# A gated graph network and an attention layer on one core: a split by a scaled rounding copy, tanh gates, a three-pass projection, and right-hand scores by way of DRAM

## The chip, the core and the metric

The kernel runs on one core of a Trainium2 chip. The metric is the device time of one execution in microseconds (us), the median of a few runs. TensorE (PE) does the matrix products, VectorE (DVE) and ScalarE (ACT) the elementwise work, GpSimd (POOL) little, and SyncE (SP) issues nearly all DMAs. Each engine works through its own queue in order.

## The reference, cut to what matters

There are 64 graphs of 256 nodes with 256 features. The first layer is a gated network of three rounds, the second an attention layer; both work on a normalised input and add to it.

```python
h = jnp.maximum(_layernorm(x, axis=-1), 0.0)
for i in range(3):                                   # gated network
    m = jnp.einsum('bnd,de->bne', h, weight[i])
    aggr = jnp.einsum('bst,bsd->btd', A, m)          # A = (adj != 0)
    gi = aggr @ w_ih.T + b_ih;  gh = h @ w_hh.T + b_hh
    r = sigmoid(i_r + h_r);  z = sigmoid(i_z + h_z)
    n = tanh(i_n + r * h_n)
    h = (1.0 - z) * n + z * h
x = x + h
h = jnp.maximum(_layernorm(x, axis=-1), 0.0)
hW = jnp.einsum('bnd,od->bno', h, W)                 # attention
e = (hW @ a_left)[:, :, None] + (hW @ a_right)[:, None, :]
e = where(adj == 0, -1e9, leaky(e))
x = x + softmax(e) @ hW
```

## The kernel before

**Pairs.** Two graphs make a pair, so that the free size of a tile is 512 columns (two graphs of 256 nodes) on 128 partitions; 32 pairs follow each other. In the gated network the features are on partitions (`hT`, two blocks `db`), in the attention layer the nodes are.

**Set-up.** `setup` (L325) transposes the weights, multiplies `weight[i]` into `w_ih`, and splits each gate matrix into three factors `fac` (`factors`, L372): a top part cut to few mantissa bits, the remainder scaled by 4096, and a correction. `wT` is W transposed, in plain float32. `va` holds W^T times the two halves of `a`, so that the attention scores are dot products with `h` itself.

**A round.** `split` (L445) takes a value apart in the same way: a cut by a bit mask on DVE (`cut`, L322), a rounding copy of the cut value on ACT (L449), the remainder on DVE (L450) and a combination of both on DVE (L451). The three parts are float32r tiles ("round" buffers). Propagation (`prop`, L584) multiplies two-part features with A into a PSUM bank; ACT copies the bank to SBUF (L588) and `split` works on the copy. `gate` (L455) then makes each gate's bank in two steps: "top" matmuls with the first two parts (L464), a scaling of the bank by 1 + 1/4096 on ACT (L478), and "rest" matmuls with the third part (L469). ACT applies the sigmoid for r (L599) and z (L610) and the tanh for n (L607); DVE multiplies r into the bank (`u`, L603), adds (L606), and mixes old and new h (L615 to L617). A DMA transpose (`dma_turn`, L489, with gathers at L494, and a joining copy on ACT at L502) brings h back to nodes on partitions for the next propagation, where `hi` (L641) and `lo` (L642) split it in two.

**The attention layer.** DVE makes the score dot products (L656) into columns of a small tile. The right-hand scores, one per node and so one per partition, are needed along the free axis on every partition: PE transposes each column, broadcast to 128 columns, into a bank `pR` (`right`, L667). ACT adds the left-hand score and applies the leaky slope (L671), DVE masks (L674) and takes the row maximum (L676). One planned operation `exps` (L679) makes the exponentials of both graphs (L683), with the sums. The result is transposed by DMA (on PE in the last pair), PE multiplies h by it (`mix`, L714, plain float32), ACT copies the bank (L718), PE multiplies by `wT` (`project`, L723, plain float32), DVE scales by the softmax sum and adds the residual (L728), and SP stores.

**The order.** A planner (`Plan`) gets every operation with its engine, an estimated occupation and latency, and the buffers that it reads and writes. It simulates the engines and emits one order for each engine's queue by least start time, then by due time, which the dictionary `LEAD` shifts by name. Buffers come from classes: "full" (28 float32 tiles), "round" (32), and "bank" (8 PSUM banks) among them. A window of four pairs may be in work at once.

Of the kernel before, what the change touches and what calls it, by code (L numbers as in the profile page):

```python
# [27 lines left out]
    "w load": 28000, "w copy": -12000, "w cut": -5000, "w 1": -17000, "w copies": -7000, "G": -9000, "G copy": -5400,  # L28
    "va copy": 4000, "in 0 stats": 5000, "in 1 relu": 10000, "turn copy 0": -11800, "h0 0": 17000, "h0 d": 13000,
    "h1 0": 36000, "prop 0": 11200, "g0 cut": 3000, "g1 cut": 13000, "g1 0": -28000, "r 0 topT": 51000,  # L30
    "r 0 rest": -4300, "r 0": 29000, "ni 0 rest": 46000, "z 0 topF": -48000, "z 0": 11000, "d mul 0": -19000,
    "r 1 topT": -34000, "r 1 rest": -1000, "nh 1 topF": -42000, "nh 1 scale": -38000, "nh 1 rest": 3000,
    "ni 1 topF": -24000, "tanh 1": 10000, "z 1 topF": -61000, "z 1 scale": -112000, "z 1": 6000, "back 0": -36000,
    "hi 0": 28000, "back copy 1": -67000, "hi 1": 52000, "mid 0 stats": -14000, "right 0": -8000,
    "mid 1 eps": -23000, "mid 1 relu": 9000, "dot 1": -31000, "mix 0": -28000, "p copy 1": 40000,
    "project 1": -6000, "turn 1 gather": 2000,
# [16 lines left out]
class Plan:  # L53
# [6 lines left out]
    def __init__(self, window, lead):  # L60
        self.ops, self.slots, self.window, self.pair = [], {}, window, -1
        self.writer, self.readers = {}, {}
        self.due = None
        self.stage = None
        self.lead = lead
        self.keep = {"full": 0, "round": 0}
# [4 lines left out]
    def op(self, name, eng, occ, lat, fn, r=(), w=(), ahead=0, port=False):  # L71
# [3 lines left out]
        o.stage, o.name, o.lead = self.stage, name, self.lead.get(name, 0)  # L75
# [125 lines left out]
def tile_gated_gnn_then_gat(  # L201
# [34 lines left out]

    nc = tc.nc
# [16 lines left out]
    plan.slot_class("full", [const.tile([P, GN], F32, name=f"full{i}") for i in range(28)])  # L254
# [4 lines left out]
    plan.slot_class("bank", [psum.tile([P, GN], F32, name=f"bank{i}") for i in range(8)])  # L259

# [28 lines left out]
    A512, V512, S512, VP256, C512 = 475, 605, 660, 392, 522  # L289
    CUT = -4096  # L290
    SPLIT = 4096.0
    C = 1.0 / SPLIT

# [4 lines left out]
    b_rz = const.tile([P, EB], F32, name="b_rz")  # L298
    b_i = vec[:, 2 * DB : 2 * DB + EB]
# [3 lines left out]
    wT = const.tile([P, DB, D], F32, name="wT")  # L303
# [21 lines left out]
    def setup():  # L325
# [16 lines left out]
        dve("b_rz", 70, lambda: nc.vector.tensor_add(b_rz, b_i, b_h), r=[("vec", ONE)], w=[("b_rz", ONE)])  # L342

# [10 lines left out]
        def transposed(dst, region, blocks):  # L354

            def go_for(c):
                pt = Buf("bank")

                def go():
                    for r, (b, k) in enumerate(blocks):  # L360
                        nc.tensor.transpose(pt.t[:, ts(r, P)], parts(b)[:, k, ts(c, P)], ident)

                n = len(blocks)
                pe("w turn", TR * n, go, r=[(b, ONE) for b, _ in blocks] + [("ident", ONE)], w=[(pt, ONE)])
                act("w copy", 140 + n * 110, lambda: nc.scalar.copy(dst(c), pt.t[:, : n * P]), r=[(pt, ONE)], w=[region(c)])

            for c in range(DB):
                go_for(c)

        H = E3 // 2  # L370

        def factors(m, T):  # L372

            def one(kb, half):
                f = lambda j: fac[m][:, j, kb, ts(half, H)]
                b, t = T[kb][half], Buf("full")
                src, top = lambda: b.t[:, :H], lambda: t.t[:, :H]
                key = (f"fac{m}", ((kb, half),))
                cut("w cut", top, src, H, [(b, ONE)], [(t, ONE)])
                dve2("w 1", 460, lambda: nc.vector.tensor_sub(src(), src(), top()), r=[(t, ONE)], w=[(b, ONE)])  # L380

                def copies():
                    nc.scalar.copy(f(0), top())
                    nc.scalar.activation(f(1), src(), AF.Copy, scale=SPLIT)

                act("w copies", 800, copies, r=[(b, ONE), (t, ONE)], w=[(f"fac{m}", ((kb, half, 0),))])
                dve2("w d", 510, lambda: nc.vector.scalar_tensor_tensor(f(2), top(), -C, src(), op0=ALU.mult, op1=ALU.add),
                    r=[(b, ONE), (t, ONE)], w=[(f"fac{m}", ((kb, half, 1),))])

            for half in range(2):  # L390
                for kb in range(DB):
                    one(kb, half)
# [4 lines left out]
        def whole(T, blocks):  # L397
            for half in range(2):
                transposed(lambda c, half=half: T[c][half].t[:, :H], lambda c, half=half: (T[c][half], ONE),
                           blocks[3 * half : 3 * half + 3])  # L400
# [4 lines left out]
        whole(whhT, whh_n)  # L405
# [24 lines left out]
        transposed(lambda c: wT[:, c, :], lambda c: ("wT", (c,)), W_n)  # L430
# [12 lines left out]
    WT = [("wT", (0, 1))]  # L443

    def split(name, v):  # L445

        t, v0, v1, vd = Buf("full"), Buf("round"), Buf("round"), Buf("round")
        cut(name + " cut", lambda: t.t, lambda: v.t, GN, [(v, ALL)], [(t, ONE)])
        act(name + " 0", C512, lambda: nc.scalar.copy(v0.t, t.t), r=[(t, ONE)], w=[(v0, ONE)])  # L449
        dve2(name + " 1", V512, lambda: nc.vector.tensor_sub(v1.t, v.t, t.t), r=[(v, ALL), (t, ONE)], w=[(v1, ONE)])  # L450
        dve2(name + " d", V512, lambda: nc.vector.scalar_tensor_tensor(vd.t, v1.t.bitcast(F32), -SPLIT, t.t, op0=ALU.mult, op1=ALU.add),  # L451
            r=[(v1, ONE), (t, ONE)], w=[(vd, ONE)])
        return v0, v1, vd

    def gate(name, e, terms, tops, apart=False, bias=0.0):  # L455
# [22 lines left out]
        act(name + " scale", 575 if "nh" in name else A512, lambda: nc.scalar.activation(bank.t, bank.t, AF.Identity, bias=bias, scale=1.0 + C),  # L478
# [4 lines left out]
    def dma_turn(name, src, t, gathers):  # L483
# [5 lines left out]
        plan.op(name, "SP", 1370, 3500, lambda: nc.sync.dma_start_transpose(  # L489
# [6 lines left out]
        for region, dst, blocks in gathers:  # L496
            plan.op(name + " gather", "SP", 1320, 4300 if blocks == slice(None) else 3100, lambda dst=dst, blocks=blocks: gather(dst, blocks),
# [11 lines left out]
    def norm_relu(name, src, dst):  # L509
# [11 lines left out]
        dve(name + " stats", 995, stats, r=[(src, ALL)], w=[(sm, (0, 1))])  # L521
# [13 lines left out]
    def pair(p):  # L535
        plan.pair = p

# [33 lines left out]
        for i in range(L):  # L571
# [4 lines left out]
            for db in range(DB):  # L576
                pa, ag = Buf("bank"), Buf("full")
# [10 lines left out]
                act(f"prop copy {db}", A512, lambda pa=pa, ag=ag: nc.scalar.copy(ag.t, pa.t), r=[(pa, ONE)], w=[(ag, ALL)])  # L588
                gs.append(split(f"g{db}", ag))
# [5 lines left out]
            for db in range(DB):  # L595
# [3 lines left out]
                act(f"r {db}", 575, lambda b=r_, k=pr, db=db: nc.scalar.activation(b.t, k.t, AF.Sigmoid, bias=b_rz[:, db : db + 1]),  # L599
                    r=[(pr, ONE), ("b_rz", ONE)], w=[(r_, ONE)])  # L600
                en = 2 * DB + db
                ph = gate(f"nh {db}", en, [("hh", hs)], tops, bias=b_h[:, en : en + 1])
                dve(f"u {db}", V512, lambda u=u, k=ph, b=r_: nc.vector.tensor_mul(u.t, k.t, b.t),  # L603
                    r=[(ph, ONE), (r_, ONE)], w=[(u, ONE)])
# [6 lines left out]
                    b.t, k.t, AF.Sigmoid, bias=b_rz[:, DB + db : DB + db + 1]),  # L611
# [4 lines left out]
                dve2(f"d mul {db}", V512, lambda d=d, b=z_: nc.vector.tensor_mul(d.t, d.t, b.t), r=[(z_, ONE)], w=[(d, ALL)])  # L616
                dve2(f"d add {db}", V512, lambda u=u, d=d: nc.vector.tensor_add(d.t, d.t, u.t), r=[(u, ONE)], w=[(d, ALL)])  # L617
# [31 lines left out]
        for g in range(G):  # L649
# [12 lines left out]
            pR = Buf("bank")  # L662

            def right(sm=sm, pR=pR):
                for nb in range(NB):
                    c = 12 + NB + nb
                    nc.tensor.transpose(pR.t[:, ts(nb, P)], sm.t[:, c : c + 1].to_broadcast([P, P]), ident)  # L667

            pe(f"right {g}", 2 * TR, right, r=[(sm, (14, 15))], w=[(pR, ONE)])
            for nb in range(NB):  # L670
                act(f"leaky {g}", 365, lambda b=sc[g], nb=nb, pR=pR, sm=sm: nc.scalar.activation(  # L671
                    parts(b)[:, nb, :], pR.t[:, :N], AF.Prelu, bias=sm.t[:, 12 + nb : 13 + nb], alpha=LEAKY_SLOPE),
                    r=[(pR, ONE), (sm, (12 + nb,))], w=[(sc[g], (nb,))])
# [5 lines left out]
        def exps():  # L679
            for g in range(G):  # L680
                s = sms[g].t
                for k in range(NB):
                    nc.scalar.activation(parts(pm_[g])[:, k, :], parts(pm_[g])[:, k, :], AF.Exp, bias=s[:, k : k + 1],  # L683
                                         accum_out=s[:, 4 + k : 5 + k])

        plan.op("exps", "ACT", 4 * 490 + 2600, 4 * 490 + 1300 + 200, exps, r=[(s, ONE) for s in sms],
                w=[(b, ALL) for b in pm_] + [(s, (1,)) for s in sms])

        for g in range(G):
# [3 lines left out]
            pT, pg, ag, pv = Buf("full"), Buf("bank"), Buf("full"), Buf("bank")  # L693
# [24 lines left out]
            act(f"mix copy {g}", A512, lambda ag=ag, pg=pg: nc.scalar.copy(ag.t, pg.t), r=[(pg, ONE)], w=[(ag, ONE)])  # L718

            def project(ag=ag, pv=pv):  # L720
                for ib in range(NB):
                    for db in range(DB):
# [45 lines left out]
```

## Time and profile before

| what | us |
|---|---|
| median of 3 runs | 2126.16 (2124.05 to 2127.03) |
| the profiled execution | 2126.64 |
| its span, first to last instruction | 2124.9 |
| mean granted TensorE clock | 0.991 |

The costliest groups, from the list by line with shapes kept apart (mean ns of one; the idle time is that of the engine just before):

| line | what | count | busy us | mean ns |
|---|---|---|---|---|
| L464 PE | top matmuls, `fac` and `fac_hh`, 512 columns | 4608 | 1242.0 | 398 |
| L469 PE | rest matmuls, 512 columns | 2304 | 712.7 | 398 |
| L584 PE | propagation, 256 columns | 1536 | 217.2 | 287 |
| L714 PE | mix, 256 columns | 512 | 126.5 | 392 |
| L723 PE | projection, 256 columns | 512 | 115.9 | 379 |
| L478 ACT | scale of a gate's bank (two forms) | 768 | 467.3 | 592, 665 |
| L502 ACT | joining copy after a DMA transpose | 310 | 363.2 | 1172 |
| L449 ACT | first part of a split | 384 | 239.5 | 631 |
| L588 ACT | copy of the propagation's bank | 192 | 113.5 | 591 |
| ACT | table loads (L683, L599 and two single ones) | 65 | 83.4 | 1283 |
| L450, L451 DVE | second and third part of a split | 768 | 507.4 | 684, 682 |
| L322 DVE | the cut of a split | 384 | 158.7 | 420 |

PE's records overlap, because matmuls are pipelined: a busy time is not a sum of what they cost, and prices are better taken from the distance between starts. Records of plain float32 matmuls come twice for each matmul of the program. A chain of waits follows the work that ended last back from release to release.

### The profile page before, as it was taken

To read this page: it belongs to the slowest core of one execution; us is meant where nothing else is said; L and a number is where in the kernel's file an instruction comes from. 1 tells how busy PE (TensorE), PEld (TensorE's weight loads), DVE (VectorE), ACT (ScalarE), POOL (GpSimd) and SP (SyncE) were. 2 spreads that over 40 slices of the span, in tenths; PEclk is the share of its full clock that TensorE was granted. 3 is DMA by queue.
4 is the path that set the end of the run, shared out by engine and by line. 5 is a ranking of instruction groups with operands and counts; after the bars stand their busy time and mean duration, and the time that the engine had idled before them with its cause. 6 is when DMAs were issued, how large, how long until landed. Compare 5 with 4: busy or idle time off the path is not lost.

```text
span 2124.9 us, 31090 instructions
## 1 busy us (share of the span) xinstructions
PE 2084.8 (98%) x9737; PEld 1712.9 (81%) x9737; DVE 1780.2 (84%) x4148; ACT 1892.6 (89%) x3255; POOL 142.9 (7%) x198
## 2 busy tenths in 40 slices
PE   8999999999999999999999999999999999999997
PEld 6787888888888888888888888888888888888875
DVE  7787888888888888888888888888888888888775
ACT  7788999999998999998999999999999989999865
POOL 1000000000000000000000000000000000000000
PEclk9999999999999999999999999999999999999998
DMA  3456765656765546766546665556765657665531
GB/s 99 75 105 119 139 117 104 103 108 127 135 118 97 107 110 129 134 119 96 109 110 129 132 120 101 104 112 127 134 118 97 108 108 131 130 119 90 91 59 40
DMA packets 729254, 234.35 MB, mean 110 GB/s; under 512 B 660977, under 2 KB 729089, under 8 KB 729089
## 3 DMA queue, kind: packets, MB, share of 16 engines
q1 hardware_dynamic: 729056, 232.36, 58.0%
q8 instruction: 77, 1.26, 0.3%
q14 instruction: 89, 0.72, 0.1%
q10 hardware_dynamic: 32, 0.01, 0.0%
HBM read 52.96 MB, written 16.78 MB: 33 GB/s over the span
## 4 chain that ended last, share of the span: by engine, by line
PE 78%; ACT 9%; DMA 6%; SPq 3%; DVE 2%; issue 2%; ACTq 0%; DVEq 0%
PE bank L464 39%; PE bank L469 19%; PE bank L584 7%; PE bank L714 6%; DMA full<-full 5%; PE bank L723 5%; SPq L494 3%; ACT full L502 2%; ACT bank L478 2%; ACT full L683 1%; ACT round L449 1%; ACT L683 1%; PE bank L421 1%; PE bank L667 1%; ACT full L599 0%
## 5 line engine op out<-in xcount | busy, mean ns | idle before, releaser
L464 PE MATMUL bank<-round,fac 128*128 128x512 f32 x2304 | 624.1, 399 | 1.9 <-ACT round L449 1.7
L464 PE MATMUL bank<-round,fac_hh 128*128 128x512 f32 x2304 | 617.9, 397 | 3.7 <-ACT round L449 3.6
L464 PEld LDWEIGHTS bank<-round,fac_hh 128*128 128x128 f32 x2304 | 432.8, 189 | 105.8 <-ACT round L449 4.8
L464 PEld LDWEIGHTS bank<-round,fac 128*128 128x128 f32 x2304 | 431.9, 189 | 101.8 <-ACT round L449 2.1
L478 ACT ACTIVATE bank<-bank 128x512 f32<-128x512 f32 x576 | 339.6, 592 | 48.3 <-PE bank L464 46.1
L502 ACT COPY full<-full 128x1024 uint16<-128x1024 uint16 x310 | 363.2, 1172 | 20.8 <-DMA full<-full 15.5
L469 PE MATMUL bank<-round,fac_hh 128*128 128x512 f32 x1152 | 356.2, 399 | 2.4 <-ACT bank L478 1.9
L469 PE MATMUL bank<-round,fac 128*128 128x512 f32 x1152 | 356.5, 396 | 0.5 <-ACT bank L478 0.5
L450 DVE TENSOR_TENSOR round<-full,full 128x512 fp32r<-128x512 f32 x384 | 255.2, 684 | 1.7
L469 PEld LDWEIGHTS bank<-round,fac 128*128 128x128 f32 x1152 | 214.4, 188 | 51.1 <-ACT bank L478 2.9
L469 PEld LDWEIGHTS bank<-round,fac_hh 128*128 128x128 f32 x1152 | 208.4, 189 | 57.6 <-ACT bank L478 16.6
L451 DVE SCALAR_TENSOR_TENSOR round<-round,full 128x512 fp32r<-128x512 f32 x384 | 252.2, 682 | 0.9 <-PE bank L464 0.5
L449 ACT CAST round<-full 128x512 fp32r<-128x512 f32 x384 | 239.5, 631 | 8.5 <-DVE full L322 5.6
L603 DVE TENSOR_TENSOR full<-bank,full 128x512 f32<-128x512 f32 x192 | 131.8, 687 | 114.2 <-ACT full L599 107.9
L524 POOL TENSOR_TENSOR small<-small,nhalf 128x2 f32<-128x2 f32 x128 | 106.2, 839 | 1787.7 <-DVE small L522 1785.5
L584 PEld LDWEIGHTS bank<-round,round 128*128 128x128 f32 x1536 | 206.1, 190 | 17.9 <-DVE round L642 2.7
L584 PE MATMUL bank<-round,round 128*128 128x256 f32 x1536 | 217.2, 287 | 3.4 <-DVE round L642 1.9
L610 ACT ACTIVATE full<-bank,b_rz 128x512 f32<-128x512 f32 x192 | 131.7, 687 | 88.8 <-PE bank L469 88.7
L615 DVE TENSOR_TENSOR full<-full,full 128x512 f32<-128x512 f32 x192 | 132.2, 689 | 75.2 <-ACT full L607 71.9
L322 DVE TENSOR_SCALAR full<-full 128x512 int32<-128x512 int32 (+1 forms) x400 | 163.7, 418 | 17.2 <-ACT full L588 8.8
L616 DVE TENSOR_TENSOR full<-full,full 128x512 f32<-128x512 f32 x192 | 131.8, 688 | 42.6 <-ACT full L610 41.9
L478 ACT ACTIVATE bank<-bank,vec 128x512 f32<-128x512 f32 x192 | 127.7, 665 | 13.1 <-PE bank L464 13.0
(78 smaller groups left out, 2407.6 us busy)
## 6 DMA issues: line engine op xcount, KB each, us to landing
full<-full SPq DMA_DIRECT2D x496, 128.0 KB, 3.5
x<-in_x_dram SPq DMA_DIRECT2D x64, 256.0 KB, 3.3
adj<-in_adj_dram SPq DMA_DIRECT2D x64, 256.0 KB, 3.1
full<-in_x_dram SPq DMA_DIRECT2D x64, 256.0 KB, 3.0
out_dram<-full SPq DMA_DIRECT2D x64, 256.0 KB, 2.4
full<-full SPq DMA_DIRECT2D x248, 64.0 KB, 2.2
full<-full SPq DMA_TRANSPOSE x310, 3.1
full<-in_L_gnn_w_ih_dram SPq DMA_DIRECT2D x3, 256.0 KB, 2.8
```

The lines of the kernel that those rows point to most:

```text
L322: dve2(name, 60 + n * 0.54, lambda: nc.vector.tensor_scalar(dst().bitcast(I32), src().bitcast(I32), CUT, None, op0=ALU.bitwise_and), r=r, w=w)
L449: act(name + " 0", C512, lambda: nc.scalar.copy(v0.t, t.t), r=[(t, ONE)], w=[(v0, ONE)])
L450: dve2(name + " 1", V512, lambda: nc.vector.tensor_sub(v1.t, v.t, t.t), r=[(v, ALL), (t, ONE)], w=[(v1, ONE)])
L451: dve2(name + " d", V512, lambda: nc.vector.scalar_tensor_tensor(vd.t, v1.t.bitcast(F32), -SPLIT, t.t, op0=ALU.mult, op1=ALU.add), r=[(v1, ...
L464: nc.tensor.matmul(bank.t, f(m, j, kb), b.t, start=(first and n == 0), stop=True, skip_group_check=True)
L469: nc.tensor.matmul(bank.t, f(m, 2, kb), s[kb][2].t, start=False, stop=True, skip_group_check=True)
L478: act(name + " scale", 575 if "nh" in name else A512, lambda: nc.scalar.activation(bank.t, bank.t, AF.Identity, bias=bias, scale=1.0 + C), ...
L502: act(name, 1065, lambda: nc.scalar.copy(dst.t.bitcast(U16).rearrange("p (j n b) -> p j n b", j=2, b=2), src.t.bitcast(U16).rearrange(f"p ...
L584: nc.tensor.matmul(pa.t[:, ts(g, N)], b, parts(A[g])[:, sb, :], start=(n == 0), stop=(n == len(terms) - 1))
L603: dve(f"u {db}", V512, lambda u=u, k=ph, b=r_: nc.vector.tensor_mul(u.t, k.t, b.t), r=[(ph, ONE), (r_, ONE)], w=[(u, ONE)])
L615: dve2(f"d sub {db}", V512, lambda u=u, d=d: nc.vector.tensor_sub(d.t, d.t, u.t), r=[(u, ONE)], w=[(d, ALL)])
L616: dve2(f"d mul {db}", V512, lambda d=d, b=z_: nc.vector.tensor_mul(d.t, d.t, b.t), r=[(z_, ONE)], w=[(d, ALL)])
```

## The change

**The split** no longer cuts by a bit mask. ACT makes the first part in one step, a copy scaled by `BELOW` = 1 - 1/8192 whose float32r output rounds; DVE takes the remainder from it, and the combination as before. For the propagated value the copy and the remainder read the PSUM bank itself, so `prop copy` and its SBUF buffer are gone.

**Tanh gates.** sigmoid(v) is written as (1 + tanh(v/2))/2. The functions at r and z become tanh with scale 0.5 and a halved bias. The n third of `w_hh` and its bias are halved at set-up, so that `u` = (tanh + 1) times the bank is r * h_n; `d mul` and `d add` take the +1 and the half of z.

**Three-pass projection.** W is split into three factors at set-up (`fac["W"]`). After `mix` the bank is split from PSUM (`c0`, `c1`), and `project` runs like a gate: first two parts, a scale of the bank on ACT, third part.

**Right-hand scores.** For all pairs but the last, a DMA writes the two score columns (8 bytes of each partition) to a row in DRAM, and a second one spreads the row to all partitions of a "full" tile; `leaky` reads that. The last pair keeps the PE transposes.

**Besides.** `exps` becomes one ACT operation for each graph, "full" has 26 tiles in place of 28, some of the planner's estimates differ, names in the first and last pair get a prefix, and `LEAD` has other entries.

```diff
+    dram = ctx.enter_context(tc.tile_pool(name="dram", bufs=1, space=bass.MemoryType.DRAM))
+    plan.slot_class("line", [dram.tile([1, N], F32, name=f"line{i}") for i in range(4)])
...
     C = 1.0 / SPLIT
+    BELOW = 1.0 - C / 2
...
-    wT = const.tile([P, DB, D], F32, name="wT")
+    fac["W"] = const.tile([P, 3, DB, D], F32R, name="fac_W")
...
-    def split(name, v):
-
-        t, v0, v1, vd = Buf("full"), Buf("round"), Buf("round"), Buf("round")
-        cut(name + " cut", lambda: t.t, lambda: v.t, GN, [(v, ALL)], [(t, ONE)])
-        act(name + " 0", C512, lambda: nc.scalar.copy(v0.t, t.t), r=[(t, ONE)], w=[(v0, ONE)])
-        dve2(name + " 1", V512, lambda: nc.vector.tensor_sub(v1.t, v.t, t.t), r=[(v, ALL), (t, ONE)], w=[(v1, ONE)])
-        dve2(name + " d", V512, lambda: nc.vector.scalar_tensor_tensor(vd.t, v1.t.bitcast(F32), -SPLIT, t.t, op0=ALU.mult, op1=ALU.add),
-            r=[(v1, ONE), (t, ONE)], w=[(vd, ONE)])
+    def split(name, v, bank=False):
+
+        v0, v1, vd = Buf("round"), Buf("round"), Buf("round")
+        act(name + " 0", A512 if bank else C512, lambda: nc.scalar.activation(v0.t, v.t, AF.Copy, scale=BELOW), r=[(v, ALL)], w=[(v0, ONE)])
+        (dve if bank else dve2)(name + " 1", V512, lambda: nc.vector.tensor_sub(v1.t, v.t, v0.t.bitcast(F32)),
+                                r=[(v, ALL), (v0, ONE)], w=[(v1, ONE)])
+        dve2(name + " d", V512, lambda: nc.vector.scalar_tensor_tensor(
+            vd.t, v1.t.bitcast(F32), -SPLIT, v0.t.bitcast(F32), op0=ALU.mult, op1=ALU.add),
+            r=[(v0, ONE), (v1, ONE)], w=[(vd, ONE)])
...
-                act(f"prop copy {db}", A512, lambda pa=pa, ag=ag: nc.scalar.copy(ag.t, pa.t), r=[(pa, ONE)], w=[(ag, ALL)])
-                gs.append(split(f"g{db}", ag))
+                gs.append(split(f"g{db}", pa, True))
...
-                act(f"r {db}", 575, lambda b=r_, k=pr, db=db: nc.scalar.activation(b.t, k.t, AF.Sigmoid, bias=b_rz[:, db : db + 1]),
+                act(f"r {db}", 575, lambda b=r_, k=pr, db=db: nc.scalar.activation(
+                    b.t, k.t, AF.Tanh, bias=b_rz[:, db : db + 1], scale=0.5),
...
-                dve(f"u {db}", V512, lambda u=u, k=ph, b=r_: nc.vector.tensor_mul(u.t, k.t, b.t),
-                    r=[(ph, ONE), (r_, ONE)], w=[(u, ONE)])
+                dve(f"u {db}", S512, lambda u=u, k=ph, b=r_: nc.vector.scalar_tensor_tensor(
+                    u.t, b.t, 1.0, k.t, op0=ALU.add, op1=ALU.mult), r=[(ph, ONE), (r_, ONE)], w=[(u, ONE)])
...
-            pR = Buf("bank")
...
-            pe(f"right {g}", 2 * TR, right, r=[(sm, (14, 15))], w=[(pR, ONE)])
+            if p < NPAIR - 1:
+                line, pR = Buf("line"), Buf("full")
+                plan.op(f"line {g}", "SP", 420, LINE, lambda line=line, sm=sm: nc.sync.dma_start(
+                    line.t.rearrange("o (q k) -> (o q) k", k=NB), sm.t[:, 12 + NB : 12 + 2 * NB]),
+                    r=[(sm, (14, 15))], w=[(line, ONE)])
+                plan.op(f"right {g}", "SP", 420, SPREAD, lambda line=line, pR=pR: nc.sync.dma_start(
+                    pR.t[:, :N], line.t.to_broadcast([P, N])), r=[(line, ONE)], w=[(pR, ONE)])
...
-            act(f"mix copy {g}", A512, lambda ag=ag, pg=pg: nc.scalar.copy(ag.t, pg.t), r=[(pg, ONE)], w=[(ag, ONE)])
-
-            def project(ag=ag, pv=pv):
-                for ib in range(NB):
-                    for db in range(DB):
-                        nc.tensor.matmul(pv.t[:, ts(ib, D)], ag.t[:, db * N + ib * P : db * N + (ib + 1) * P],
-                                         wT[:, db, :], start=(db == 0), stop=(db == DB - 1))
-
-            pe(f"project {g}", 4 * MM, project, r=[(ag, ONE)] + WT, w=[(pv, ONE)])
+            cs = split(f"c{g}", pg, True)
+
+            def project(js, first, cs=cs, pv=pv):
+                for n, (ib, db, j) in enumerate((ib, db, j) for ib in range(NB) for db in range(DB) for j in js):
+                    nc.tensor.matmul(pv.t[:, ts(ib, D)], cs[j].t[:, db * N + ib * P : db * N + (ib + 1) * P],
+                                     fac["W"][:, j, db, :], start=(first and n == 0), stop=True, skip_group_check=True)
+
+            pe(f"project {g}", 8 * PROP, lambda project=project: project((0, 1), True),
+               r=[(cs[0], ONE), (cs[1], ONE), ("facW", ((0, 0), (1, 0)))], w=[(pv, ONE)])
+            act(f"project {g} scale", A512, lambda pv=pv: nc.scalar.activation(pv.t, pv.t, AF.Copy, scale=1.0 + C), w=[(pv, ONE)])
+            pe(f"project {g} rest", 4 * PROP, lambda project=project: project((2,), False),
+               r=[(cs[2], ONE), ("facW", ((0, 1), (1, 1)))], w=[(pv, ONE)])
```

## The prediction

> **What bounds the kernel now.** I read the page's busy totals first, with the row of busy tenths and the granted clock.
>
> ```profile
> PE 2084.8 (98%) x9737; PEld 1712.9 (81%) x9737; DVE 1780.2 (84%) x4148; ACT 1892.6 (89%) x3255; POOL 142.9 (7%) x198
> PE   8999999999999999999999999999999999999997
> PEclk9999999999999999999999999999999999999998
> ```
>
> TensorE is busy in every slice at almost its whole clock; ScalarE follows at 89%. Overlapping matmuls flatter a busy PE, so I checked with start-to-start distances: the PE timeline, by the projection's matmuls in two successive pairs.
>
> ```profile
> 1069.47 3.62 PE L723 MATMUL bank<-wT,full 128*128 128x256 f32 x16
> 1133.24 3.62 PE L723 MATMUL bank<-wT,full 128*128 128x256 f32 x16
> ```
>
> One pair takes 63.8 us here. From the projection at 237.22 us to that at 1898.87 us lie 26 pairs, 63.91 us each. The chain of waits in order of time (start, us, what) prices each kind of PE work:
>
> ```profile
> 1067.90 1.73 PE bank L714 x8
> 1069.63 3.45 PE bank L723 x16
> 1087.55 0.95 PE bank L584 x8
> 1103.40 4.65 PE bank L464 x20
> 1108.98 0.44 PE bank L667 x4
> ```
>
> A gate matmul (L464, L469) costs 4.65/20 = 0.2325 us, a propagation matmul (L584: round operands, 256 columns) 0.119 us. A projection of one graph is 4 program matmuls, recorded as 8, at 3.45/2 = 1.725 us. The right-hand transposes of a pair (L667) cost 0.44 us. PE work per pair: 216 gate matmuls 50.22, 48 propagations 5.71, two mixes 3.46, two projections 3.45, right-hand scores 0.44: 63.28 us. The shortest periods are 63.30 and 63.31, so the sum is the floor, and the mean period is 0.63 us above it. **PE is the bound in the steady part**, and work taken from PE is worth its full price there. The list of waits says what makes the excess (us in total, times, longest):
>
> ```profile
> ACT full L502 <- DMA full<-full: 15.5, 22, 1.6
> PE bank L714 <- ACT full L502: 8.1, 15, 1.3
> PE bank L469 <- ACT bank L478: 2.4, 6, 0.5
> ```
>
> **Edit 1, projection in three passes.** Per graph it becomes 12 matmuls of the form that L584 has (round operands, 128x128 weights, 256 columns). 12 x 0.119 = 1.425 us against 1.725, so 0.30 us less, times 64: **-19.2 us**. The nearest row is exact in shape and type, so I take it.
>
> Its cost elsewhere: a scale of the bank on ScalarE between the passes (64 x 0.592 by L478 = 37.9 us), and two DVE operations per graph for the split of the mixed value (128 x 0.683 by L450 and L451 = 87.4 us). The first ScalarE split replaces the copy at L718 one for one. All of it runs under other pairs' gates. The new handoff PE to ACT to PE is the one that every gate has: 768 such handoffs cost PE 2.4 us in the list above, so 64 more cost 0.2 us. Behind the waiting scale stand other gates' scales and tanhs on ScalarE's queue; at the worst each would stall for scale and signal, 0.8 us, 51 us in all. The gates are the near row, so 0.2.
>
> **Edit 2, right-hand scores through DRAM, pairs 0 to 30.** 31 x 0.44 = **-13.6 us** of PE. Added per graph: two DMAs on SP's queue, a store of 8 bytes from each of 128 partitions and a load that spreads 1 KB to 128 partitions. Issue is about 0.6 us each (the L494 rows: 0.62 median), so 2.5 us per pair. SP's issues now take about 10 transposes x 1.27 + 24 gathers x 0.62 + 8 loads and stores x 0.57 = 32 us of 64, so the queue has room.
>
> Latency: the rows that are near are the 256 KB store to DRAM, 2.4 us to landing, and loads from DRAM, 3.0 to 3.3. With issues: 0.6 + 2.4 + 0.6 + 3.0 = 6.6 us, where two transposes took some 0.4. **A rule that speaks against this**: the Trainium skill, "DMA: Bandwidth & Descriptors", section "Anatomy of one DMA", puts a fixed 2 us on each transfer whatever its size, mostly the receipt of the write, heaviest towards HBM; its rules for authors say that transfers under 64 KB are mostly overhead. By that rule an estimate is 2 x 2.0 + issues = 5.2 us, by the rows 6.6: either way over ten times the PE price in latency, and it is paid before leaky, mask, max and exps of that graph. But it is latency, not PE time: PE has up to four pairs in the plan's window to work on, and pair 31, which has no cover, keeps the transposes. I cost it at nothing; if the cover were gone it would cost 2 x 6.2 us in each of 31 pairs at most. From below it can't gain beyond the PE time.
>
> What is queued behind it: `right` waits on SP for `line` to land, and behind it wait the L489 transposes and L494 gathers of other pairs, whose data the gates (by `hi`, `lo`) and the mix need. That is the rival below.
>
> **Edit 3, tanh for the sigmoids.** The ScalarE timeline in a steady pair:
>
> ```profile
> 1050.04 1.28 ACT L683 ACT_TABLE_LOAD   x1
> 1055.56 0.71 ACT L607 ACTIVATE full<-full,vec 128x512 f32<-128x512 f32 x1
> 1058.44 1.28 ACT L599 ACT_TABLE_LOAD   x1
> ```
>
> After the table load for the exponentials a tanh (L607) runs without another load; the next load comes only before the sigmoid. So tanh lives in the exponential's table, and without sigmoids the 63 or 64 switching loads go: 63 x 1.283 = 80.8 us of ScalarE. Here rule and row differ in size: the Trainium skill, "ScalarE: Activation LUTs", section "What ACT_TABLE_LOAD costs", adds a drain of 1.38 us and budgets 2.66 us for a switch, which would be 168 us. The trace has the load at 1.28 and hundredths of a us around it (the operation before ends at 1050.01), so I use 81. Worth on PE: ScalarE is not the bound, but one load stands in the chain exps, DMA transpose, L502, mix that ends the 8.1 us wait above.
>
> The halved weights and biases are set up once: eight ScalarE parts and two short DVE operations, about 1 us, beside PE's set-up matmuls. `u`, `d mul` and `d add` keep their count as two-operation forms: L451 against L450 shows no difference (682 and 684 ns); from a bank it may be 0.06 us more (L728 476 ns against L656 420, a pointer among the causes), so `u` adds 0 to 11 us of DVE.
>
> **Edit 4, the split.** Removed: 384 cuts (L322, 420 ns: 158.7 us DVE) and 192 propagation copies (L588, 591 ns: 113.5 us ACT). The first part becomes a scaled copy, for g straight from the bank: 0.591 (L588) in place of 0.631 (L449), for h 0 to 0.02 more (L384 against L383): -8 to -4 us together. DVE reads g from PSUM as it does at L606 (681 ns): no change. The bank is held through DVE's read, about 0.9 us longer, six times a pair; the pair's two right-hand banks are free.
>
> Sums: ACT 1892.6 - 113.5 - 80.8 + 37.9 - 6 = 1730 us; DVE 1780.2 - 158.7 + 87.4 + 11 = 1720 us. Over about 2088 us both stand at 83 and 82%: **PE stays the bound**, with more slack beside it. From propagation to gate the chain loses a copy, a cut and two signals: 0.59 + 0.42 + 0.3 = 1.3 us.
>
> **Stalls that can go.** Steady: 26 x 0.63 = 16 us of excess, of which the mix wait is the visible half. The exponentials lose a load and are split by graph, so the first transpose starts 2 to 3 us sooner; but the planner places every engine afresh with a new set of leads, and the L494 DMA's time to landing (2.1 to 6.3 us) stays. Bounds 0 and -16; I take -3. Start (to 170 us): idle of 3.44 + 1.67 + 0.81 + 1.19 us and small ones, all ending at a split's cast, `hi` or `lo`; the shorter chain takes 0 to 6; I take -3. End: the chain shows L683's loads at 2080.37 and 2105.48 and L599's at 2083.77 ahead of PE waits of 2.20 and 2.93 us: -3.5. Against it, the last projection now has c0, c1 and the scale in a row where one copy was: 0.59 + 0.84 + 0.76 + waits, less the shorter passes: +1. New handoffs, SP's waits and bank holding: between 0 and 15, taken as +3, since the same mechanisms cost PE little now.
>
> **The sum** against the profiled execution (2126.64 us, span 2124.9): 2126.6 - 19.2 - 13.6 - 3 - 3 - 3.5 + 1 + 3 = 2088.3. The median is 0.5 below it: **2088 us**, -1.8%. A measurement of this kernel tells about 0.2%, 4.3 us, from no change.
>
> **Rivals.**
> A, the forecast: PE's work and a few stalls go; 2078 to 2098. Chance 0.57.
> B, the slack on ACT and DVE removes most of the steady excess too: 2126.6 - 32.8 - 16 - 6 = 2072 (2060 to 2078). For it: the four shortest periods sit on the floor already. Against: the mix wait hangs on DMAs that nothing shortens. 0.15.
> C, half the gain is eaten by new waits (banks held longer, two `full` buffers fewer while scores wait 6 us for DRAM): 0.6 us per pair back, 2088 + 20 = 2108 (2098 to 2118). For it: `hb`, `sc`, the masked buffer and the residual of each graph live 6 us longer, 8 x 6.2 = 50 buffer-us per pair, and `pR` adds some; against: the cut's 12 and the copies' 8 buffers per pair, of 4 us or so, are no longer needed. 0.20.
> D, **slower**: SP stands at `right` until `line` has landed, 2.4 us twice a pair, with a ready transpose behind it, and PE has nothing else to run: 4.8 - 1.04 = 3.8 us per pair, 31 x 3.8 = 117: about 2240. It decides from a stall of 1.3 us per pair on (40/31), a quarter of that wait. For: SP is in order, and mix has no slack. Against: SP's own list of waits has 564.9 us for `d add` (L617) alone, so it mostly has nothing ready, and other gates cover. 0.05, with 0.03 left for no change within 0.2%.
> E, that the loads stay (tanh placed in another table than the exponential's): ACT at 87%, +4 us; inside C. L607 speaks against it.
>
> The range to hold eight in ten takes A whole, most of B and half of C: 2068 to 2110. Chances: faster 0.92, within 0.2% 0.03, slower 0.05.
>
> **What would show it.** Right: projection rows at 12 matmuls, 1.43 us per graph start to start; transposes for right-hand scores only in the last pair; period 62.3 to 62.9 us; one or two table loads in all; ACT near 1730, DVE near 1720. Wrong: PE idle before L714 or the gates growing behind L494 or L489; SP waiting long at the spread; a bank wait at propagation; DVE above 90%.

## The result and the profile after

The changed kernel takes **2089.5 us** (median of 4 runs, 2087.34 to 2090.49) against 2126.6 for the kernel before beside it: ratio 0.9827, 95% interval 0.981 to 0.9844. That is 1.7% faster, some 37 us; 2088 was forecast. The page of its profiled execution (2089.78 us, span 2088.0), busy totals, tenths of PE and granted clock, and the DMA queue (packets, MB, share of the 16 engines):

```profile
PE 2053.6 (98%) x9869; PEld 1691.6 (81%) x9869; DVE 1737.0 (83%) x3900; ACT 1768.0 (85%) x3069; POOL 159.4 (8%) x198
PE   8999999999999999999999999999999999999997
PEclk9999999999999999999999999999999999999998
...
q1 hardware_dynamic: 746912, 240.56, 65.8%
```

Two rows of the list of DMA issues are new, the spread and the store of the right-hand scores (count, KB each, median us from issue to landing):

```profile
full<-line SPq DMA_DIRECT2D x62, 128.0 KB, 4.2
...
line<-small SPq DMA_DIRECT2D x62, 1.0 KB, 4.3
```

PE is still the one full engine. ACT fell by 125 us of busy time, DVE by 43. The PE timeline (start, us, then the group) at the first projection of two successive pairs, and the chain of waits between them (start, us, what):

```profile
1063.85 1.12 PE L756 MATMUL bank<-fac_W,round 128*128 128x256 f32 x8
1126.22 1.12 PE L756 MATMUL bank<-fac_W,round 128*128 128x256 f32 x8
```

```profile
1058.70 3.45 PE bank L748 x16
1062.15 1.86 PE bank L486 x8
1064.01 0.95 PE bank L756 x8
1064.96 0.93 PE bank L486 x4
1065.89 1.43 PE bank L756 x12
1067.32 0.95 PE bank L607 x8
1068.27 0.47 PE bank L756 x4
```

This is a pair at the floor: 62.37 us, with no row but PE's in its chain. The two mixes (L748) still cost 3.45 us; the two projections (L756) now cost 0.95 + 1.43 + 0.47 = 2.85 us where they cost 3.45, and no transposes of scores stand in it. Over 26 pairs (projection at 243.27 to that at 1882.79 us) the mean period is 63.06 us, 0.69 above that shortest one. The waits of PE and of its weight loads (us in total, times, longest) and the group of table loads (count, busy, mean ns, idle before):

```profile
PEld bank L491 <- ACT bank L500: 20.7, 78, 3.1
PE bank L491 <- ACT bank L500: 5.3, 5, 2.7
PEld bank L756 <- DVE round L470: 4.9, 13, 0.5
PEld bank L748 <- ACT full L524: 4.8, 8, 1.3
PEld bank L756 <- ACT bank L761: 4.3, 20, 0.5
```

```profile
L382 ACT ACT_TABLE_LOAD x1 | 1.3, 1283 | 2.0 <-issue 2.0
```

The wait of the mix for its transposed input (16.9 us of weight loads before) is down to 4.8. In its place the projection waits, which it never did before: for its split on DVE and for the scale of its bank on ACT, 9.2 us together. Of 65 table loads one is left.

**Where the 37 us of span come from.** Steady part: 26 pairs x (63.91 - 63.06) = 22.1 us. Everything before and after it (six pairs, start and end): 237.22 + 2124.9 - 1898.87 = 463.3 us before, 243.27 + 2088.0 - 1882.79 = 448.5 after, 14.8 us less. The cut lies at the projection in both, which may stand a few us earlier or later in its pair.

A count of PE's work separates this better. Take each matmul record of both traces at its start-to-start price (0.2325 and 0.119 us for round operands, 0.216 for half a plain float32 matmul, 0.109 for a score transpose, medians for the set-up). PE's work is then 2056.4 us before and 2023.7 after, **32.7 us less**. What the span has beyond that work:

| beyond PE's priced work, us | before | after |
|---|---|---|
| up to the second pair's projection | 25.4 | 18.5 |
| 26 pairs | 16.4 | 21.2 |
| after them | 26.7 | 24.6 |
| whole span | 68.5 | 64.3 |

So nearly all of the gain is PE work that is gone. The waits outside it moved in both directions and ended 4.2 us lower. At the start the granted clock (0.96 and 0.99 up to the cut) is part of it: PE ran at half clock for 17.1 us before and for 6.8 after, by an estimate worth 5 us at most.

### The profile page after: what moved, and what is told of

The parts are those of the page before. It is cut to its first block, busy times and chain, and to the rows that moved or that the text cites. A ratio compares the mean times of both kernels' runs of the same rounds, so it can differ in the third digit from the quotient of the medians.

```text
span 2088.0 us, 31193 instructions
## 1 busy us (share of the span) xinstructions
PE 2053.6 (98%) x9869; PEld 1691.6 (81%) x9869; DVE 1737.0 (83%) x3900; ACT 1768.0 (85%) x3069; POOL 159.4 (8%) x198
## 3 DMA queue, kind: packets, MB, share of 16 engines
q1 hardware_dynamic: 746912, 240.56, 65.8%
q8 instruction: 78, 1.28, 0.3%
## 4 chain that ended last, share of the span: by engine, by line
PE 80%; DVE 7%; DMA 6%; ACT 4%; issue 1%; SPq 1%; DVEq 0%; ACTq 0%
PE bank L486 42%; PE bank L491 21%; PE bank L607 7%; DMA full<-full 6%; PE bank L756 4%; PE bank L748 4%; DVE round L470 2%; DVE round L472 1%; ACT full L524 1%; ACT full L552 1%; PE bank L441 1%; DVE full L710 1%; DVE small L712 1%; DVE full L639 1%; DVE small L539 1%
## 5 line engine op out<-in xcount | busy, mean ns | idle before, releaser
L486 PE MATMUL bank<-round,fac_hh 128*128 128x512 f32 x2304 | 614.5, 399 | 3.2 <-ACT round L469 1.9
L524 ACT COPY full<-full 128x1024 uint16<-128x1024 uint16 x310 | 360.8, 1165 | 34.4 <-DMA full<-full 23.0
L491 PE MATMUL bank<-round,fac_hh 128*128 128x512 f32 x1152 | 348.9, 397 | 5.5 <-ACT bank L500 5.3
L472 DVE SCALAR_TENSOR_TENSOR round<-round,round 128x512 fp32r<-128x512 f32 x448 | 307.1, 686 | 5.6
L546 POOL TENSOR_TENSOR small<-small,nhalf 128x2 f32<-128x2 f32 x128 | 125.5, 989 | 1736.3 <-DVE small L544 1683.6
L491 PEld LDWEIGHTS bank<-round,fac_hh 128*128 128x128 f32 x1152 | 206.3, 188 | 54.9 <-ACT bank L500 14.8
L470 DVE TENSOR_TENSOR round<-bank,round 128x512 fp32r<-128x512 f32 x256 | 176.0, 687 | 69.3 <-ACT round L469 65.9
L629 DVE TENSOR_TENSOR full<-full,bank 128x512 f32<-128x512 f32 x192 | 130.9, 682 | 80.1 <-PE bank L491 72.7
L469 ACT ACTIVATE round<-bank 128x512 fp32r<-128x512 f32 x256 | 148.7, 594 | 44.4 <-PE bank L607 37.2
L630 ACT ACTIVATE full<-full,vec 128x512 f32<-128x512 f32 x192 | 138.6, 722 | 45.2 <-DVE full L629 23.9
L639 DVE SCALAR_TENSOR_TENSOR full<-full,full 128x512 f32<-128x512 f32 x192 | 130.2, 678 | 34.0 <-ACT full L633 34.0
L626 DVE SCALAR_TENSOR_TENSOR full<-full,bank 128x512 f32<-128x512 f32 x192 | 131.2, 683 | 29.7 <-ACT full L621 29.4
L667 DVE TENSOR_TENSOR round<-full,round 128x512 fp32r<-128x512 f32 x124 | 85.3, 688 | 73.0 <-ACT round L666 73.0
```

The lines of the kernel that those rows point to most:

```text
L469: act(name + " 0", A512 if bank else C512, lambda: nc.scalar.activation(v0.t, v.t, AF.Copy, scale=BELOW), r=[(v, ALL)], w=[(v0, ONE)])
L470: (dve if bank else dve2)(name + " 1", V512, lambda: nc.vector.tensor_sub(v1.t, v.t, v0.t.bitcast(F32)), r=[(v, ALL), (v0, ONE)], w=[(v1, ...
L486: nc.tensor.matmul(bank.t, f(m, j, kb), b.t, start=(first and n == 0), stop=True, skip_group_check=True)
L491: nc.tensor.matmul(bank.t, f(m, 2, kb), s[kb][2].t, start=False, stop=True, skip_group_check=True)
L524: act(name, 1065, lambda: nc.scalar.copy(dst.t.bitcast(U16).rearrange("p (j n b) -> p j n b", j=2, b=2), src.t.bitcast(U16).rearrange(f"p ...
L626: dve(f"u {db}", S512, lambda u=u, k=ph, b=r_: nc.vector.scalar_tensor_tensor(u.t, b.t, 1.0, k.t, op0=ALU.add, op1=ALU.mult), r=[(ph, ONE) ...
```

## Experiments

All changes below are to the changed kernel unless said otherwise. Each kernel ran beside the kernel before; "+" is the difference of its ratio from 0.9827, times 2124 us. Intervals are about 0.15% to each side, so differences under some 5 us aren't told apart.

| run | ratio to the kernel before | against the changed kernel |
|---|---|---|
| e1, scores on PE, planned afresh | 0.9995 (0.9986 to 1.0005) | +36 us |
| e2, plain projection | 0.9865 (0.9849 to 0.9880) | +8 us |
| e3, sigmoids, order kept | 1.0012 (1.0006 to 1.0019) | +39 us |
| e4, spread twice, order kept | 1.0106 (1.0091 to 1.0121) | +59 us |
| e5, old split, planned afresh | 1.0407 (1.0392 to 1.0423) | +123 us |
| e6, kernel before, no leads | 1.1185 (1.1165 to 1.1205) | |
| e7, changed kernel, no leads | 1.0699 (1.0681 to 1.0717) | +185 us |
| e8, mix in three products, planned afresh | 1.0196 (1.0181 to 1.0211) | +78 us |
| f1, as e1, leads fitted | 0.9833 (0.9814 to 0.9853) | +1 us |
| f3, sigmoids, leads fitted | 0.9866 (0.9848 to 0.9884) | +8 us |
| f5, as e5, leads fitted | 1.0019 (1.0012 to 1.0027) | +41 us |
| f4, two-part splits, leads fitted | 0.9744 (0.9719 to 0.9768) | -18 us |

**e1: the scores back on PE.** Edit: the branch that goes through DRAM is never taken.

```diff
-            if p < NPAIR - 1:
+            if False:
                 line, pR = Buf("line"), Buf("full")
```

> The changed kernel with the right-hand scores of all pairs back on PE transposes into a bank; the planner places the operations afresh. Theory 1 (PE work at full price): 31 x 0.44 = 13.6 us more, 2103. Rival 2 (the way through DRAM has a cost of its own in waits of SP's queue and in buffers held longer): less than half of that comes back, 2090 to 2096.

Measured: +36 us, more than either theory gave. The periods wander from 61.5 to 67.3 us round a mean of 63.84. The planner had made a new order with leads that belong to another program; this and not the transposes may be what was measured. f1 below settles it.

**e2: a plain projection in almost the same order.** The first part of the projection's split becomes a plain copy; its two DVE parts and the scale of the bank emit nothing.

```diff
-            cs = split(f"c{g}", pg, True)
+            cs = split(f"c{g}", pg, True, True)
...
-                for n, (ib, db, j) in enumerate(...):
-                    nc.tensor.matmul(pv..., cs[j]..., fac["W"][:, j, db, :], ...)
+                for ib in range(NB if first else 0):
+                    for db in range(DB):
+                        nc.tensor.matmul(pv..., cs[0]..., wT[:, db, :], ...)
```

> The changed kernel with the projection in plain float32 again: one copy of the mixed bank, 4 float32 matmuls per graph, no scale, no split of the mixed value; the planner still believes in the three passes, so the order stays nearly the same. Theory 1: 64 x 0.30 = 19.2 us more, 2108.7, although ACT loses some 36 us and DVE 88 us of work. Rival (slack on ACT and DVE matters): their relief gives half or more of it back, under 2099.

Measured: +8 us by the ratio, 4.8 by the medians (2094.27): the rival's answer. Yet the floor did what theory 1 says. The PE timeline of e2 at the projections of two pairs:

```profile
1003.84 1.89 PE L761 MATMUL bank<-fac_W,full 128*128 128x256 f32 x8
1066.85 1.89 PE L761 MATMUL bank<-fac_W,full 128*128 128x256 f32 x8
```

63.01 us, and the shortest of all periods is 63.00: 0.63 above the changed kernel's 62.37, as 2 x 0.30 asks. But the mean is only 63.27, so the excess over the floor is 0.27 us instead of 0.69. **Three passes take 0.6 us from PE's floor in each pair and give some 0.4 back** in waits for the new split and scale.

**e3: table loads back, order kept.** `AF.Tanh` becomes `AF.Sigmoid` at r and z; nothing else.

> The changed kernel with the function Sigmoid in place of Tanh at r and z, everything else and the order of all engines unchanged, so that only the table loads come back (the gates' values are other ones: the computation differs in r and z). Theory 1: some 63 loads x 1.283 = 81 us of ACT that PE hardly sees, 0 to 6 us more, 2090 to 2096. Rival (the loads stand in the chain exps, transpose, mix that PE waits for): 1.3 to 2.6 us per pair, 40 to 80 us more, 2130 to 2170.

Measured: +39 us. Its list of waits:

```profile
PEld bank L491 <- ACT bank L500: 80.2, 165, 3.1
PE bank L491 <- ACT bank L500: 34.4, 64, 2.7
```

A load of 1.28 us that the order doesn't know of delays the scales behind it on ACT's queue, and the "rest" matmuls wait for those: PE idles 34.4 us there against 5.3. The rival had the wrong place (no wait of the mix is among the large ones of this list), but near the right size. Most periods are 63.80 or just above: 1.43 us over the floor in every pair. The mean is 0.84 above the changed kernel's, 22 of the 39 us; the rest falls to the pairs at the start and the end.

**e4: the spread issued twice.** One list comprehension round the DMA, two issues.

> The changed kernel with the spreading DMA issued twice in a row onto the same tile, order unchanged, so that the second waits on SP for the first to land and the scores come one landing (4.2 us) and one issue later. Theory 1 (latency before leaky is covered): 0 to 6 us more, 2090 to 2096. Rival (SP standing before a DMA holds back the transposes behind it, and PE runs dry): a good part of 62 x 4.8 = 298 us, at least 2120.

Measured: +59 us, 0.95 us for each of 62 graphs. The second issue starts 3.3 us after the first (median), but from the store's start to that of `leaky` the way grew by 1.8 us on average, from 10.1 to 11.8. The group of `leaky` in the changed kernel and in e4, and e4's list of waits:

```profile
L707 ACT ACTIVATE full<-full,small 128x256 f32<-128x256 f32 x124 | 61.2, 522 | 1.9 <-DMA full<-line 1.8
L707 ACT ACTIVATE full<-full,small 128x256 f32<-128x256 f32 x124 | 61.4, 523 | 63.7 <-DMA full<-line 63.4
```

```profile
ACT full L707 <- DMA full<-line: 63.4, 38, 3.2
...
PEld bank L486 <- DVE round L470: 32.9, 33, 1.1
...
PE bank L491 <- ACT bank L500: 25.1, 27, 2.7
```

`leaky` (L707) stands at the head of ACT's queue until the scores land, and everything behind it on ACT (scales, splits) comes late. In the changed kernel ACT waits 1.8 us in all for the scores, so there the order has left room for the latency; a little more and it is felt. What PE loses comes mostly through ACT's queue: PE's wait before the mix, which transposes held back on SP would lengthen, is 3.6 us in all against 2.2.

**e5: the old split**, with cuts on DVE and the copies of the propagation's and the mix's bank, planned afresh.

> The changed kernel with the old split: the cut on DVE, then the rounding copy, and copies of the propagation's and the mix's bank to SBUF first; the planner places afresh. PE's work is the same. Theory 1: ACT gains back 256 copies (some 120 us at 0.48 us start to start) and DVE 448 cuts (some 160 us), which brings both near 90 per cent: 0 to 15 us more, 2090 to 2105. Rival (slack on ACT and DVE and the shorter chain are what keeps PE fed): more than 15 us, towards 2120.

+123 us, periods from 51 to 82 us. Again a misfitting order may be part of it; f5 below repeats this edit.

**e6 and e7: no leads.** `Plan(WINDOW, {})` in both kernels.

> The kernel before with an empty LEAD, so with the planner's own order. Beside the next run. Theory 1 (the gain is PE work): slower than 2126 by some tens of us, and the changed kernel with an empty LEAD lies 25 to 45 us below it. Rival 3 (the gain is in the new leads, the order): the two without leads lie within 15 us of each other, or the changed one is the slower.

> The changed kernel with an empty LEAD. Theory 1: 25 to 45 us below the kernel before with an empty LEAD, and slower than 2089.5. Rival 3: within 15 us of it, or slower.

They take 2375.6 and 2272.0 us, 104 apart: outside both theories. The change is not only an order (rival 3 falls: without leads it gains more), but leads are worth 252 and 185 us, seven and five times what the change is. Part of that is clock: the mean granted clock is 0.966 in e6 and 0.980 in e7, against 0.991 and 0.994 with leads. Counted as lost time that is some 81 and 45 us (an estimate, span times the missing share), so up to 35 of the 104 us between the two. **An undo that is planned afresh under foreign leads can measure mostly its order**, as e1 against f1 and e5 against f5 show. The last four kernels carry leads fitted to each by a search over the end that the planner itself computes, from the changed kernel's leads.

No run has the changed kernel, or the kernel before, after that same search. What these four show against the changed kernel is therefore the edit together with whatever the search alone may bring. An undo can cost more than its number says, and f4's edit gain less; how much isn't known.

**e8: the mix in round operands too**, under foreign leads; the product of the two remainders is left out.

> The changed kernel with the mix, too, in round operands: h and the transposed exponentials are each split in two (a rounding copy on ACT, a remainder on DVE), and three of the four products are made, 12 matmuls of 0.119 us in place of 4 of 0.43 per graph; the product of the two remainders is left out. Theory 1: 64 x 0.30 = 19.2 us less, 2070, with ACT and DVE some 64 and 77 us longer (about 88 per cent). Rival (slack on ACT and DVE matters): the gain is eaten, 2080 or more.

+78 us, uninformative for the same reason; its idea is taken up in f4.

**f1: the scores on PE, leads fitted.**

> The first undo again (right-hand scores of all pairs on PE), with a LEAD that was fitted to it by a search over the planner's own estimate of the end, starting from the changed kernel's. Theory O (the excess of the undo over its PE time was an order that did not fit): 13.6 us of PE more, about 2103, 2098 to 2108. Rival S (the way through DRAM frees banks and slack that a refitted order can't replace): it stays at 2115 or more.

Neither. It is +1 us by the ratio (2087.59 by the median, 2 less): against the changed kernel's order, the 13.6 us of PE work show no cost. The PE timeline at two projections, and the only large wait of PE's side:

```profile
984.28 1.31 PE L819 MATMUL bank<-fac_W,round 128*128 128x256 f32 x8
1047.15 1.31 PE L819 MATMUL bank<-fac_W,round 128*128 128x256 f32 x8
```

```profile
PEld bank L554 <- ACT bank L563: 22.4, 111, 1.1
```

The common period is 62.84 to 62.87, the changed kernel's floor plus the 0.44 us of transposes, and the mean over the same 26 pairs is 62.96: PE runs almost without a gap. **So the way through DRAM saves 0.44 us of PE in each pair, and the kernel that has it sits 0.69 above its floor where this one sits 0.12 above.**

Where the changed kernel waits can be read from the start-to-start distances of PE in the 26 pairs, each less the median distance of its line. Before the projection PE starts late by 0.30 us per pair in the changed kernel, by 0.42 in f3, 0.17 in f5 and 0.56 in f4: these have both the three passes (f4 its own three products) and the way through DRAM. There is no delay in f1, which lacks the way, and 0.01 in e2, which lacks the passes. But e1 lacks the way too and has 0.24 under its foreign leads, so an order alone can make such a wait. The way was not taken out under the changed kernel's order, and the part that it plays stays open.

**f3: sigmoids, leads fitted**, with both graphs' exponentials in one planned operation.

> The changed kernel with sigmoids (biases and factors of two put right, exponentials of both graphs in one operation whose table loads the planner is told of) and a LEAD fitted to it. ACT has some 63 loads, 81 us, more. Theory O: a planned load costs PE little, 2090 to 2103. Rival S: ACT's load is felt whatever the order, 2115 or more as with the unplanned loads.

+8 us: theory O. Its busy totals:

```profile
PE 2054.4 (98%) x9869; PEld 1684.7 (81%) x9869; DVE 1746.5 (83%) x3900; ACT 1841.0 (88%) x3133; POOL 136.7 (7%) x198
```

Loads that the planner is told of, in an order fitted to them, cost a fifth of what unplanned ones cost in e3, though ACT carries them all the same.

**f5: the old split, leads fitted.**

> The old split with its copies and cuts, and a LEAD fitted to it. PE's work is that of the changed kernel, ACT and DVE have 125 and 145 us more. Theory O: 2095 to 2112. Rival S: ACT and DVE at 86 per cent keep PE waiting whatever the order, 2130 or more.

+41 us: 2127.3 by the median, 2130 by the ratio, so at the edge of S. Its busy totals and largest waits:

```profile
PE 2072.8 (98%) x9869; PEld 1683.4 (79%) x9869; DVE 1888.0 (89%) x4348; ACT 1891.4 (89%) x3325; POOL 150.6 (7%) x198
```

```profile
PEld bank L555 <- ACT bank L564: 53.2, 167, 1.9
PEld bank L813 <- ACT full L588: 14.6, 28, 1.3
PE bank L555 <- ACT bank L564: 13.3, 34, 1.5
```

PE has exactly the changed kernel's matmuls (9869 records). With ACT and DVE both at 89%, the scales come late and the mean period over the 26 pairs is 64.43, 2.1 us above the changed kernel's floor. PE's late start before the "rest" matmuls, reckoned as in f1, is 1.17 us per pair against 0.20 in the changed kernel. **The new split takes nothing from PE, and undone alone it costs the most of the four edits.** This is its worth beside the other three: with the projection's old split in it, f5 loads DVE with 108 us more than the kernel before had. How much of the 41 us a longer search would recover isn't known.

**f4: two-part splits.** Each value is split in two, three products of the parts are made in one pass, and the product of the remainders is left out, in gates, projection and mix. The scale and "rest" steps stay for nh alone, with its bias.

```diff
-        v0, v1, vd = Buf("round"), Buf("round"), Buf("round")
+        v0, v1 = Buf("round"), Buf("round")
...
+    THREE = ((0, 0), (0, 1), (1, 0))
-            seq = [(m, j, kb, s[kb][j]) for m, s in terms for kb in range(DB) for j in range(2)]
+            seq = [(m, j, kb, s[kb][q]) for m, s in terms for j, q in THREE for kb in range(DB)]
...
-        act(name + " scale", ...)
-        pe(name + " rest", ...)
```

> A version after the experiments: every split in two parts instead of three (a rounding copy and the remainder), three of the four products of the parts in one pass for gates, projection and mix, the product of the two remainders left out; no scale of a bank but for nh, no third part; a LEAD fitted to it. PE has 19.2 us less (mix in round operands), ACT and DVE some 300 and 250 us less. Theory O with slack: PE's floor of 61.8 us per pair with little above it, 2045 to 2062. Rival (what lies above the floor comes from DMAs and waits that slack doesn't touch): 2068 to 2075.

2070.16 us by the median, 0.9744 of the kernel before: the fastest of all, 2.6% (2.3 to 2.8) under the kernel before, and the rival's number. Its busy totals and two waits:

```profile
PE 2032.2 (98%) x10125; PEld 1693.4 (82%) x10125; DVE 1540.0 (74%) x3562; ACT 1525.2 (74%) x2557; POOL 130.0 (6%) x198
```

```profile
PEld bank L816 <- DVE round L527: 10.7, 11, 1.4
PE bank L816 <- DVE round L527: 8.2, 8, 1.2
```

ACT and DVE went from 85 and 83 to 74%, and the gain of 18 us is no more than PE's 19.2 us of mix. The slack on top of it bought nothing that shows here; what waits now is the projection (L816) for its split. With the scores on PE as well it was not tried.

## Why the prediction was right, and where it wasn't

**PE's work: right.** 32.8 us were to go, and 32.7 are gone: the new projection's matmuls cost 0.119 us each, as the near row did. 62.24 us (63.28 - 1.04) was the sum of rows for a pair, and the shortest period measured is 62.37; e2 gives the projection's 0.60 as 0.63, f1 the transposes' 0.44 as 0.47.

**"Work taken from PE is worth its full price": right for the floor, not for the time.** The excess over the floor doesn't stay put when an edit brings its own waits. The 19.2 us of the projection are worth about 5 to 8 (e2), the 13.6 us of the scores about nothing against f1's fitted order.

**"The gates are the near row, so 0.2": the term mis-sized.** The 2.4 us were the wait of PE's own row; the weight loads' row for the same handoffs was 19.4. For the projection's scale the two rows are 0.5 and 4.3 us, and for its split on DVE, which this term left out, 1.2 and 4.9. From start to start PE comes 0.30 us late per pair, some 9 us in 31 pairs. As f1 has the same passes and no such delay, the handoff need not cost this.

**The DRAM path "at nothing": the latency was too low, the cost is open.** The time from issue to landing holds the issue, so the rows made 2.4 + 3.0 = 5.4 us, not 6.6. Store and spread took 4.3 + 4.2 = 8.5 us, 9.0 with SP's time between them. The fixed 2 us of the Trainium skill ("DMA: Bandwidth & Descriptors", "Anatomy of one DMA") gave 5.2 us as an estimate; that section works its figure out for transfers that GpSimd issues, and SP issued these. The rule warned of the right thing, and all these numbers were low. ACT waits only 1.8 us for the scores, so the direct cost was small as forecast; what the path adds before the projection is not separated. e4 shows how thin the cover is: 1.8 us later at `leaky` cost 0.95 us per graph.

**The split at "0 and -16" of stalls: the step that failed most.** It was counted as slack, and stalls were to give back 3 us. f5, which undoes it and keeps the rest, loses 41: without it the extra ACT and DVE work of the projection brings both engines to 89%, and PE waits for the scales.

**Sums of ACT and DVE: mis-sized.** 1730 and 1720 forecast, 1768.0 and 1737.0 measured. I subtracted rows' durations, but successive instructions overlap. The kernel before, ACT timeline:

```profile
1066.97 0.59 ACT L588 COPY full<-bank 128x512 f32<-128x512 f32 x1
1067.43 0.61 ACT L718 COPY full<-bank 128x512 f32<-128x512 f32 x1
```

A copy of 0.59 us is followed 0.46 us later by the next operation: taking 192 of them out frees some 0.47 us each, 23 us less in all than 192 x 0.59. That is 23 of the 38 us by which ACT was off; the rest was not followed.

**The loads: right.** One is left; told to the planner they cost 8 us (f3).

**Why the total held all the same.** The forecast was 32.8 us of PE work and 5.5 us of stalls: 3 at the start, 2.5 at the end, nothing net in the steady part. The stalls gave 4.2: 6.9 at the start, 2.1 at the end, and the steady part lost 4.8. So a pair became 0.85 us shorter where its work asked 1.04. In the steady part PE's late start before the mix fell from 0.48 to 0.17 us per pair, and one of 0.30 came up before the projection: effects of the kind of B and of C were both at work and nearly cancelled. The forecast was right on the work by its reasons, and near on the rest by luck. D (PE dry behind SP) did not happen: PE is idle for 5.4 us in the 26 pairs.

Is the gain a better fitted order rather than the edits? The count of PE's work says that 32.7 of the 37 us are work. The other 4 may be order, as neither kernel's leads are known to be the best.

## What to carry to other kernels

Take the floor of the bounding engine from start-to-start distances, and then price each edit twice: what it takes from the floor, and what it adds to the distance from the floor on the other engines' queues. In a kernel whose order is fixed in advance, an undo or an unplanned delay of one microsecond can show mostly the misfit of the order; give every variant, the starting point too, an order fitted to it by the same search before comparing. An edit that takes nothing from the full engine can carry the edits that do.

## What the runs showed of the hardware

- A store of 8 bytes from each of 128 partitions to DRAM took 4.3 us to land, more than a 256 KB store in the same trace (2.5). The Trainium skill's "DMA: Bandwidth & Descriptors" ("Specifications") says that transfers below 512 bytes are done by read-modify-write; the trace shows the time, not the cause.
- The share of DMA engine time (packets' time over the span of 16 engines) went to 65.8% from 58.0%, though the path's 62 stores and spreads carry only 3% of the bytes. But f5 and e7, which have the path, show 58.6 and 55.4%, and e6, which lacks it, 55.1%. The packets' time varies that much between orders, so no price of the path can be read from this.
- PE's granted clock was 1.00 in the 26 pairs of both kernels, where PE is busy 99% or more. In e6 and e7, where it is busy 92 and 93% of the span, the mean clock was 0.966 and 0.980. The two went together; which brought the other was not tested.
